# Layer 3 of a graph network on one core: node states by tile and slot, gates at the end of each chunk

## The chip, the core and the metric

The kernel runs on one core of one Trainium2 chip. The metric is the device time of one execution, in microseconds; the kernel before takes 39,711.06 us (median of 10 runs, 39,692.48 to 39,771.42). Five engines run their own instruction streams: TensorE (PE in the profile; its weight loads are PEld), VectorE (DVE), ScalarE (ACT), GpSimd (POOL) and SyncE (SP). Here POOL issues every indirect DMA (gathers and scatters of table rows by index) and SP every plain DMA.

## What is computed

A graph of 12,500 nodes with 32 features and 212,500 directed edges goes through four graph layers; each result is added to its input and layer-normalised. The sort of the edges, layers 0 to 2 and the norms are the same in both kernels, but for one column that layer 2 carries along. Layer 3 is the one that matters:

```python
out = relu(n_feat @ lin0_w.T + lin0_b); h = out
eh  = relu(e_feat @ en1_w.T + en1_b)                # edges x 128
w_e = (eh @ en2_w.T + en2_b).reshape(-1, 32, 32)    # one 32x32 matrix an edge
for _ in range(6):
    msg = einsum('ei,eio->eo', out[src], w_e)
    agg = segment_sum(msg, dst, 12500) + conv_bias
    h = gru_cell(relu(agg), h, gru_wih, gru_whh, gru_bih, gru_bhh)
    out = h
```

All of it is float32. The GRU cell is `r = sigmoid(ir+hr)`, `z = sigmoid(iz+hz)`, `n = tanh(in + r*hn)`, `h = (1-z)*n + z*h`.

## The kernel before

**Tiles, chunks, slots.** The edges, sorted by destination, are cut into 1,664 tiles of 128. A chunk is 32 tiles (`CB`), so a step has 52 chunks (`NCH`); a half is 16 tiles (`HB`). Within a tile the edges belong to a few consecutive destinations. A destination's number modulo 13 (`W`) is its slot, so a 0/1 mask of 128 edges by 13 slots, built on DVE (L848), turns the sum over edges into matmuls. A node whose edges run over several tiles is summed up by a scan along the tiles (L871). A table row for each (tile, slot), 1,664 x 13 = 21,632 rows (`SLOTS`), holds the running sum of that slot's node after that tile; `slot_end` tells for each node the row in which its sum is complete.

**One step.** The loop `For_i` runs six times over a step, whose body is written out for all 52 chunks (`conditioned` inside `slot_sum`). One half of a chunk is:

- POOL: 16 indirect gathers (L258) into `g`, three buffers. A row of the table `t3` has 64 floats (256 bytes): the state `h` of the source node and `h` times `en2_b`, the message's bias part.
- SP: one load of `eh`, 16 tiles by 128 floats, 1 MB, three buffers (L1064).
- Eight times, for a pair of tiles: DVE multiplies the state by the mask into `prod` (L1068, 128 x 2 x 32 x 13), PE makes two matmuls with `eh` as weights into `m` (L1076, two PSUM buffers), ACT copies `m` into `outer` (L1083).
- Then `flush()` runs the function `second` that the half before left behind: 32 matmuls with the blocks of `en2_i` into the four partition groups of `acc` (L1094), and after them 16 matmuls of `g[:, j, F:]` with the mask into the same `acc` (L1104). These are the last readers of `g`.

After the second half of a chunk comes `then()`: `on` (DVE, L858), `part` (ACT, L868/869), the scan (DVE, L871), `by8` (ACT, L881), four matmuls `back` (L888) that add the four partition groups and turn the result into rows by tile and slot, `o` (ACT, L896), and the write of the chunk's rows of `sums` (SP, L898).

**Between two steps.** When all chunks are done, 98 gathers fetch each node's row of `sums` by `slot_end` into `agg`; `conv_b` is added (L1004), relu (L1005), the array is transposed, and 25 groups go through the gates (L1012 to L1027: bias, two matmuls, sigmoid, tanh, five DVE operations, into `state`). Then `new_table` transposes the state, multiplies by `en2_b` (L227) and writes the whole of `t3` (L206). The next step's gathers wait for that write.

**Order.** Tile's scheduler sets the order of instructions on each engine from the program's order, a priority and the buffers of each pool; engines meet through semaphores. A float32 matmul leaves two matmul records and two weight-load records in the trace; a transpose one.

Of the kernel before, what the change touches and what calls it, by code (L numbers as in the profile page):

```python
# [62 lines left out]
R8 = 8 * W  # L64
SLOTS = R8 * J8
# [6 lines left out]
def tile_gnn(ctx: ExitStack, tc: tile.TileContext, a: dict, out: bass.AP):  # L72
# [95 lines left out]
    conv_b = rows("conv_b", a["L3_gnn_conv_bias"], F)  # L168

# [5 lines left out]
    for c in range(4):  # L175
# [9 lines left out]
    edge_h = dram.tile([P, J, EH], F32, name="edge_h", tag="edge_h")  # L185
    sums = [dram.tile([SLOTS + 1, F], F32, name=f"sums{i}", tag=f"sums{i}") for i in range(2)]
# [3 lines left out]
        for n, w in (("x", F), ("t0", F), ("t1p", F), ("t1q", F), ("t2a", F), ("t2b", F), ("t3", 2 * F))  # L190
    }

    with tc.tile_pool(name="zeros", bufs=1) as pool:
        zero = sb(pool, [P, P - NH, 2 * F], F32, "zero")
        nc.vector.memset(zero, 0.0)
        for s in scans:
            nc.sync.dma_start(s[EP : EP + 1, :], zero[0:1, 0, 0:F])
        for s in sums:
            nc.sync.dma_start(s[SLOTS : SLOTS + 1, :], zero[0:1, 0, 0:F])
        for t in tables.values():  # L200
            w = t.shape[1]
            nc.sync.dma_start(t.rearrange("(p c) f -> p c f", p=P)[:, NH:P, :], zero[:, :, 0:w])
# [62 lines left out]
    slot_end = sb(keep, [P, NH], I32, "slot_end")  # L265
    state = sb(keep, [P, C, F], F32, "state")
# [10 lines left out]
    def sort_edges():  # L277
        with ExitStack() as st:
# [41 lines left out]
            with tc.tile_pool(name="hist", bufs=1, space=PSUM) as psum:  # L320
                for k in ("s", "d"):
# [31 lines left out]
                    if k == "d":  # L353
# [5 lines left out]
                            run, ones[:, 0:1].to_broadcast([P, NH]), tot, initial=0.0, op0=ALU.mult, op1=ALU.add  # L359
                        )  # L360
# [101 lines left out]
    def all_of(pool, k, record, scattered):  # L462

        t = sb(pool, [1, record.shape[1]], I32, f"fence_{k}")
        i = nc.sync.dma_start(t, record[0:1, :])
        for s in scattered:
            after(i, s)
        return i
# [281 lines left out]
    with tc.tile_pool(name="dst", bufs=1) as dst:  # L750
# [31 lines left out]
        with tc.tile_pool(name="num", bufs=1) as work, tc.tile_pool(name="nump", bufs=2, space=PSUM) as psum:  # L782
# [40 lines left out]
            nc.vector.tensor_scalar(most, most, W - 0.5, None, op0=ALU.is_gt)  # L823
            nc.vector.tensor_copy(crowded, most[0:1, :])
# [13 lines left out]
    def slot_sum(name, rows, table, fill, agg):  # L838


        with tc.tile_pool(name=f"sl_{name}", bufs=2) as work, tc.tile_pool(
            name=f"slp_{name}", bufs=2, space=PSUM
        ) as psum:
            prev = [None]

            def one(c):
                mask = sb(work, [P, CB, W], F32, "mask", bufs=3)
                nc.vector.tensor_tensor(  # L848
                    mask,
                    slot[:, c * CB : (c + 1) * CB].unsqueeze(2).to_broadcast([P, CB, W]),  # L850
                    iota_w.unsqueeze(1).to_broadcast([P, CB, W]),
                    op=ALU.is_equal,
                )
                acc = sb(psum, [rows, CB, W], F32, "acc")

                def then():
                    on = sb(work, [rows, W, CB + 1], F32, "on")
                    nc.vector.tensor_tensor(  # L858
                        on,
                        going[0:rows, c, :].unsqueeze(1).to_broadcast([rows, W, CB + 1]),  # L860
                        iota_w[0:rows, :].unsqueeze(2).to_broadcast([rows, W, CB + 1]),
                        op=ALU.is_equal,
                    )
                    part_ = sb(work, [rows, W, CB + 1], F32, "part")
                    if prev[0] is None:
                        nc.vector.memset(part_[:, :, 0:1], 0.0)
                    else:
                        nc.vector.tensor_copy(part_[:, :, 0], prev[0][:, :, CB])  # L868
                    nc.scalar.activation(part_[:, :, 1:], acc.rearrange("p t w -> p w t"), AF.Copy)
                    s = sb(work, [rows, W, CB + 1], F32, "s")  # L870
                    nc.vector.tensor_tensor_scan(  # L871
                        s.rearrange("p w t -> p (w t)"),
                        on.rearrange("p w t -> p (w t)"),
                        part_.rearrange("p w t -> p (w t)"),
                        initial=0.0,
                        op0=ALU.mult,
                        op1=ALU.add,
                    )
                    prev[0] = s
                    by8 = sb(work, [rows, CB // 8, W, 8], F32, "by8")  # L880
                    nc.scalar.activation(  # L881
                        by8.rearrange("p b w t -> p w b t"),
                        s[:, :, 1:].rearrange("p w (b t) -> p w b t", t=8),
                        AF.Copy,
                    )
                    back = sb(psum, [R8, CB // 8, F], F32, "back", bufs=1)
                    for b in range(CB // 8):
                        nc.tensor.matmul(  # L888
                            back[:, b, :],
                            by8[:, b].rearrange("p w t -> p (w t)"),  # L890
                            stack[0:rows, :],
                            start=True,
                            stop=True,
                        )
                    o = sb(work, [R8, CB // 8, F], F32, "o")
                    nc.scalar.activation(o, back, AF.Copy)  # L896
                    n = CB // 8
                    nc.sync.dma_start(  # L898
                        table[0:SLOTS, :].rearrange("(r b) f -> r b f", r=R8)[:, c * n : (c + 1) * n, :], o
                    )  # L900

                fill(work, psum, c, mask, acc, then)

            for c in range(NCH):
                one(c)
            fill(None, None, None, None, None, None)
        for c in range(NH):
            gather(agg[:, c, :], table, slot_end[:, c : c + 1])
# [9 lines left out]
    def layer2(sum_into):  # L918

        with tc.tile_pool(name="n2", bufs=1) as n2:  # L920
# [5 lines left out]
            hid = node_array(n2, "hid")  # L926

            def conv(name, h, table, nr):

                own = sb(n2, [P, NH, F], F32, "own")  # L930
                nc.vector.tensor_tensor(own, h[:, 0:NH, :], wide(root), op=ALU.mult)
                write_table(table, own)
# [100 lines left out]

    def convolved(name, table, nr, agg):
        def fill(work, psum, c, mask, acc, then):
            if work is None:
                return
            g = sb(work, [P, CB, F], F32, "g", bufs=3)
            for j in range(CB):
                gather(g[:, j, :], tables[table], idx_d[:, c * CB + j : c * CB + j + 1])  # L1040
            for j in range(CB):
                nc.tensor.matmul(acc[:, j, :], g[:, j, :], mask[:, j, :], start=True, stop=True)
            then()

        slot_sum(f"l2{name}", F, sums[nr], fill, agg)

    def conditioned(agg):
        waiting = []

        def fill(work, psum, c, mask, acc, then):  # L1050
# [4 lines left out]
            if work is None:  # L1055
                flush()
                return
            for b in range(2):
                t0 = c * CB + b * HB
                g = sb(work, [P, HB, 2 * F], F32, "g", bufs=3)  # L1060
                for j in range(HB):
                    gather(g[:, j, :], tables["t3"], idx_d[:, t0 + j : t0 + j + 1])
                eh = sb(work, [P, HB, EH], F32, "eh", bufs=3)
                nc.sync.dma_start(eh, edge_h[:, t0 : t0 + HB, :])  # L1064
                outer = sb(work, [EH, F, HB, W], F32, "outer")
                for j in range(0, HB, 2):
                    prod = sb(work, [P, 2, F, W], F32, "prod")
                    nc.vector.tensor_tensor(  # L1068
                        prod,
                        g[:, j : j + 2, 0:F].unsqueeze(3).to_broadcast([P, 2, F, W]),  # L1070
                        mask[:, b * HB + j : b * HB + j + 2, :].unsqueeze(2).to_broadcast([P, 2, F, W]),
                        op=ALU.mult,
                    )
                    m = sb(psum, [EH, 2, 512], F32, "m")
                    for i in range(2):
                        nc.tensor.matmul(  # L1076
                            m[:, i, 0 : F * W],
                            eh[:, j + i, :],
                            prod[:, i].rearrange("p f w -> p (f w)"),
                            start=True,  # L1080
                            stop=True,
                        )
                    nc.scalar.activation(  # L1083
                        outer[:, :, j : j + 2, :].rearrange("k f t w -> k t f w"),
                        m[:, :, 0 : F * W].rearrange("k t (f w) -> k t f w", w=W),
                        AF.Copy,
                    )
                flush()

                def second(b=b, g=g, outer=outer):  # L1090
# [171 lines left out]
```

## Time and profile before

| | |
|---|---|
| median of 10 runs | 39,711.06 us |
| the profiled execution | 39,697.11 us |
| its span | 39,695.3 us |
| mean granted TensorE clock over the span | 0.685 |
| PE / PEld busy | 19,819.8 us (50%) / 11,203.6 us (28%) |
| POOL busy | 23,264.5 us (59%) |
| DVE / ACT busy | 10,520.9 us (27%) / 7,337.0 us (18%) |
| DMA, software queue (POOL's) | 723,584 packets, 512.50 MB |
| DMA, hardware queue (SP's) | 451,052 packets, 1,029.85 MB |
| layer 3 within the span | 22,660 to 39,640 us |

How to read it. The group lines have the source line, the engine, the operation, `out<-in` with its shape and the count; then the busy time in us and the mean ns of one; then the engine's idle time just before these instructions, and which event ended most of it. "issue" there means that the engine waited for no other engine and no transfer that the profile shows. A timeline line has the start, the duration, the engine and the work, and in brackets the idle time before it. A line by stretch has the stretch, its length, the busy time and the number of records of PE, PEld, DVE, ACT and POOL, the granted clock (1.00 is full speed; an idle PE shows 0.50), the share of the DMA engines and GB/s. L258, L1076 and the others are lines of the kernel before.

### The profile page before, as it was taken

How to read it: one execution, taken by the hardware profiler on the slowest of the kernel's cores; microseconds unless marked ns; L12 is line 12 of the kernel's file. 1: busy time of each engine (PE TensorE's matmuls, PEld its weight loads, DVE VectorE, ACT ScalarE, POOL GpSimd, SP SyncE). 2: the span in 40 equal slices, each digit the busy share in tenths (PEclk: the TensorE clock that was granted, in tenths of full speed). 3: DMA queues.
4: the chain of work that ended last, by engine and by line, in shares of the span. 5: the costliest groups of instructions: out<-in, count | busy, mean ns of one | idle time of the engine just before them, and what ended most of it. 6: DMA issues, size and time to landing. Idle time of an engine off the chain costs nothing. (4 is left out here: it accounts for less than half of the span.)

```text
span 39695.3 us, 317851 instructions
## 1 busy us (share of the span) xinstructions
PE 19819.8 (50%) x121935; PEld 11203.6 (28%) x121935; DVE 10520.9 (27%) x12313; ACT 7337.0 (18%) x11783; POOL 23264.5 (59%) x22620
## 2 busy tenths in 40 slices
PE   3555444400000003961111288688788688687786
PEld 3444433300000001221111144344344344343343
DVE  8333333310100003000000133333333333333333
ACT  0111111100000003110000033233233233232232
POOL 0444444477677773026666666566566566666665
PEclk6666666655555556555555588888888888888888
DMA  0000000011111113210000122122122122222222
GB/s 10 1 1 1 9 16 16 16 28 23 22 18 18 18 18 94 92 55 13 13 14 13 28 67 65 53 67 65 53 67 65 53 65 63 56 66 55 64 65 52
DMA packets 1176160, 1562.93 MB, mean 39 GB/s; under 512 B 663528, under 2 KB 885484, under 8 KB 1085804
## 3 DMA queue, kind: packets, MB, share of 16 engines
q1 hardware_dynamic: 451052, 1029.85, 7.9%
q0 software_dynamic: 723584, 512.50, 7.7%
q8 instruction: 989, 16.20, 0.2%
q14 instruction: 535, 4.38, 0.0%
HBM read 1257.04 MB, written 283.77 MB: 39 GB/s over the span
## 5 line engine op out<-in xcount | busy, mean ns | idle before, releaser
L258 POOL DMA_INDIRECT g<-t,idx_d x9984 | 10475.6, 1049 | 5565.2 <-issue 2795.9
L1076 PE MATMUL m<-prod,eh 128*128 128x416 f32 x19968 | 8365.9, 580 | 209.0 <-DVE prod L1068 132.5
L1068 DVE TENSOR_TENSOR prod<-g,mask 128x832 f32<-128x832 f32 x4992 | 5130.8, 1028 | 6316.3 <-PE m L1076 5898.3
L1083 ACT ACTIVATE outer<-m 128x832 f32<-128x832 f32 x4992 | 4507.8, 903 | 6540.9 <-PE m L1076 6216.3
L1076 PEld LDWEIGHTS m<-prod,eh 128*128 128x128 f32 x19968 | 3913.5, 213 | 3977.5 <-issue 2871.7
L1094 PE MATMUL acc<-outer,en_i 128*32 128x208 f32 x39936 | 3474.3, 359 | 1478.2 <-issue 1458.8
L382 POOL DMA_INDIRECT rec_s<-rows_s,pos x1664 | 1707.7, 1026 | 2730.5 <-DVE pos L432 2239.3
L258 POOL DMA_INDIRECT g<-t2a,idx_d x1664 | 1587.1, 954 | 2432.7 <-DMA t2a<-own 1652.8
L421 PE MATMUL place<-cur,xt 128*128 128x98 f32 x6652 | 1732.5, 354 | 2281.6 <-ACT cur L427 1217.2
L382 POOL DMA_INDIRECT rec_d<-record,row_d x1664 | 1654.4, 994 | 1993.0 <-DVE row_d L444 803.0
L1094 PEld LDWEIGHTS acc<-outer,en_i 128*32 128x32 f32 x39936 | 1528.9, 111 | 3426.7 <-issue 3113.6
L686 PE MATMUL t<-ident,gp 128*128 128x128 f32 x416 | 110.7, 441 | 4531.9 <-DMA gp<-t1p,rs 2888.1
L410 PE MATMUL same<-xt 128*128 128x128 f32 x6656 | 1661.9, 370 | 1309.9 <-issue 659.2
L848 DVE TENSOR_TENSOR mask<-slot,iota_w 128x416 f32<-128x416 bf16 x416 | 245.4, 591 | 7525.1 <-PE acc L1104 3109.9
L258 POOL DMA_INDIRECT gp<-t1p,rs x1664 | 1787.0, 1074 | 663.7 <-issue 556.4
L258 POOL DMA_INDIRECT g<-t,rs x1664 | 1770.8, 1064 | 532.5 <-issue 519.1
L258 POOL DMA_INDIRECT g<-t2b,idx_d x1664 | 1587.3, 954 | 831.0 <-issue 484.8
L258 POOL DMA_INDIRECT gq<-t1q,rs x1664 | 1763.9, 1060 | 510.3 <-issue 510.3
L421 PEld LDWEIGHTS place<-cur,xt 128*128 128x128 f32 x6652 | 1275.9, 239 | 2673.7 <-ACT cur L427 1513.8
L427 ACT ACTIVATE cur<-next 128x98 f32<-128x98 f32 x3326 | 838.5, 252 | 5419.5 <-PE next L422 2396.5
L888 PE MATMUL back<-stack,by 128*104 128x32 f32 (+1 forms) x3328 | 462.4, 290 | 2443.0 <-ACT by L881 2228.3
L410 PEld LDWEIGHTS same<-xt 128*128 128x128 f32 x6656 | 1228.7, 245 | 1468.3 <-ACT xt L407 767.2
(316 smaller groups left out, 19053.9 us busy)
## 6 DMA issues: line engine op xcount, KB each, us to landing
eh<-edge_h SPq DMA_DIRECT2D x624, 1024.0 KB
g<-t,idx_d POOLq DMA_INDIRECT x9984
edge_h<-eh SPq DMA_DIRECT2D x52, 2048.0 KB
scan<-o SPq DMA_DIRECT2D x104, 512.0 KB
ht<-h_t SPq DMA_DIRECT2D x104, 512.0 KB
rd<-rec_d SPq DMA_DIRECT2D x52, 544.0 KB
record<-in_edge_attr SPq DMA_DIRECT2D x52, 512.0 KB
rec_s<-rows_s,pos POOLq DMA_INDIRECT x1664
```

What stands on the lines that cost most here:

```text
L258: nc.gpsimd.indirect_dma_start(out=to, out_offset=None, in_=table, in_offset=bass.IndirectOffsetOnAxis(ap=idx, axis=0))
L382: i = nc.gpsimd.indirect_dma_start(out=to, out_offset=bass.IndirectOffsetOnAxis(ap=idx, axis=0), in_=data, in_offset=None)
L410: nc.tensor.matmul(same[:, j, :], xt[:, j, :], xt[:, j, :], start=True, stop=True)
L421: nc.tensor.matmul(place[:, j, :], xt[:, j, :], cur, start=False, stop=True)
L427: nc.scalar.activation(cur, nxt, AF.Copy)
L686: nc.tensor.transpose(t[:, g, :], gp[:, jj : jj + 4, :].rearrange("p j f -> p (j f)"), ident)
L848: nc.vector.tensor_tensor(mask, slot[:, c * CB : (c + 1) * CB].unsqueeze(2).to_broadcast([P, CB, W]), iota_w.unsqueeze(1).to_broadcast([P, ...
L888: nc.tensor.matmul(back[:, b, :], by8[:, b].rearrange("p w t -> p (w t)"), stack[0:rows, :], start=True, stop=True,)
L1068: nc.vector.tensor_tensor(prod, g[:, j : j + 2, 0:F].unsqueeze(3).to_broadcast([P, 2, F, W]), mask[:, b * HB + j : b * HB + j + 2, :].unsq ...
L1076: nc.tensor.matmul(m[:, i, 0 : F * W], eh[:, j + i, :], prod[:, i].rearrange("p f w -> p (f w)"), start=True, stop=True,)
L1083: nc.scalar.activation(outer[:, :, j : j + 2, :].rearrange("k f t w -> k t f w"), m[:, :, 0 : F * W].rearrange("k t (f w) -> k t f w", w=W ...
L1094: nc.tensor.matmul(af[q * F : (q + 1) * F, b * HW : (b + 1) * HW], en2_i[:, i, :], outer[:, i].rearrange("k t w -> k (t w)"), start=i < 4, ...
```

## The change

Layer 3 of the usual path is written anew as `layer3_tiles`; the general path for crowded graphs keeps the old `layer3`.

- The node states live in two tables, `states[0]` and `states[1]`, with a row for each (tile, slot), like `sums`. At the start `h` is scattered to `states[0]` by `slot_end` with 98 indirect DMAs, and a read that waits for all of them (`all_of`) follows. The set-up at the start of the kernel fills `states[0]` with zeros.
- The gathers of a step read these tables directly, by the row number of the source node, `idx_t`. The rows have 32 floats (128 bytes); there is no bias half. `idx_t` is made in layer 2: its tables get a 33rd column with `slot_end`, and the chunk's copy of that column is kept.
- The bias part now goes by the sum of the states: 16 mask matmuls sum the gathered states into `ssum`, ACT copies them to `ss`, the 32 matmuls with `en2_i` follow, and four matmuls with `en2_b` (`by4`) add the bias part to `acc`. In `second` the mask matmuls, the last readers of `g`, thus come first. `g` has four buffers.
- Each chunk ends with its own gates: `stack` adds the four partition groups into `ft` (by feature), relu with `conv_bias` gives `mt`, the chunk's 4 x 104 old rows (`old`, loaded by SP at the start of the chunk) are transposed to `ht`, one bias matmul and eight GRU matmuls fill `gates`, then sigmoid, tanh and five DVE operations, and SP writes the chunk's rows of the next table. Every row of the table gets a state, of running sums too; rows of unfinished sums are never gathered.
- The loop runs three times over two steps, `a` from `states[0]` to `states[1]` and `b` back. The 98 gathers by `slot_end` remain once, behind the loop.
- `m` keeps two PSUM buffers; `acc`, the sums `states`, `ft` and `gates` have one each (in the kernel before `acc` has two and `back` one).
- `crowded` is set as well when the graph has nodes without a row (`lacking`).

The core of the diff (`running` and `mask_of` hold the old lines of `slot_sum` up to `by8`, whose layout is now `b, (w t)`; the pair loop in `half` is the old one with `g[:, j : j + 2, :]`):

```diff
-        for n, w in (..., ("t2a", F), ("t2b", F), ("t3", 2 * F))
+        for n, w in (..., ("t2a", F + 1), ("t2b", F + 1), ("t3", 2 * F))
...
     def convolved(name, table, nr, agg):
+        def fill(work, c, mask, acc):
+            g = sb(work, [P, CB, F + 1], F32, "g", bufs=3)
             for j in range(CB):
                 gather(g[:, j, :], tables[table], idx_d[:, c * CB + j : c * CB + j + 1])
+            if name == "a":
+                nc.vector.tensor_copy(idx_t[:, c * CB : (c + 1) * CB], g[:, :, F])
...
+    def layer3_tiles():
...
+            for c in range(NH):
+                i = nc.gpsimd.indirect_dma_start(
+                    out=states[0],
+                    out_offset=bass.IndirectOffsetOnAxis(ap=slot_end[:, c : c + 1], axis=0),
+                    in_=h[:, c, :],
+                    in_offset=None,
+                )
...
+            all_of(n3, "states", states[0], scattered_, F32)
+
+        def gates(work, psum, c, by8, old, new):
+            t = sb(psum, [F, B8, R8], F32, "ft")
+            nc.tensor.matmul(
+                t.rearrange("f b r -> f (b r)"), stack, by8.rearrange("p b r -> p (b r)"), start=True, stop=True
+            )
+            mt = sb(work, [F, B8, R8], F32, "mt")
+            nc.scalar.activation(mt, t, AF.Relu, bias=conv_col[:, 0:1])
+            t = sb(psum, [F, B8, R8], F32, "ft")
+            for b in range(B8):
+                nc.tensor.transpose(t[:, b, :], old[:, b, :], ident[0:R8, 0:R8])
+            ht = sb(work, [F, B8, R8], F32, "ht")
+            nc.scalar.activation(ht, t, AF.Copy)
+            t = sb(psum, [R8, B8, 4, F], F32, "gates")
+            nc.tensor.matmul(
+                t.rearrange("r b k f -> r (b k f)"), ones2[:, 0:R8],
+                gru_b.rearrange("b c k f -> b (c k f)"), start=True, stop=False, skip_group_check=True,
+            )
+            for b in range(B8):
+                tb = t[:, b].rearrange("r k f -> r (k f)")
+                nc.tensor.matmul(tb, mt[:, b, :], gru_i[0:F, 0, :], start=False, stop=False, skip_group_check=True)
+                nc.tensor.matmul(tb, ht[:, b, :], gru_h[0:F, 0, :], start=False, stop=True, skip_group_check=True)
+            rz = sb(work, [R8, B8, 2, F], F32, "rz")
+            nc.scalar.activation(rz, t[:, :, 0:2, :], AF.Sigmoid)
...
+            nc.sync.dma_start(by_chunk(new, c), d)
+
+        def step(k, old_, new):
...
+                def half(c, b, mask, old, sums_):
+                    t0 = c * CB + b * HB
+                    g = sb(work, [P, HB, F], F32, "g", bufs=4)
+                    for j in range(HB):
+                        gather(g[:, j, :], old_, idx_t[:, t0 + j : t0 + j + 1])
...
+                    flush()
+
+                    def second():
+                        if b == 0:
+                            sums_.append(sb(psum, [P, CB, W], F32, "acc"))
+                            sums_.append(sb(psum, [P, GC, W], F32, "states"))
+                        acc, ssum = sums_
+                        for j in range(HB):
+                            q = j % 4
+                            nc.tensor.matmul(
+                                ssum[q * F : (q + 1) * F, b * HB // 4 + j // 4, :],
+                                g[:, j, :], mask[:, b * HB + j, :], start=True, stop=True,
+                            )
+                        n = HB // 4
+                        ss = sb(work, [P, n, W], F32, "ss")
+                        nc.scalar.activation(ss, ssum[:, b * n : (b + 1) * n, :], AF.Copy)
+                        af = acc.rearrange("p t w -> p (t w)")
+                        for i in range(F):
...
+                        by4 = acc.rearrange("p (g q) w -> p g q w", q=4)
+                        for q in range(4):
+                            nc.tensor.matmul(
+                                by4[q * F : (q + 1) * F, b * n : (b + 1) * n, q, :],
+                                en2_b[q * F : (q + 1) * F, q, :], ss[q * F : (q + 1) * F],
+                                start=False, stop=True, skip_group_check=True,
+                            )
+                        if b == 1:
+                            prev[0], by8 = running(work, P, c, acc, prev[0])
+                            gates(work, psum, c, by8, old, new)
+
+                    waiting.append(second)
+
+                for c in range(NCH):
+                    mask = mask_of(work, c)
+                    old = sb(work, [R8, B8, F], F32, "old", bufs=3)
+                    nc.sync.dma_start(old, by_chunk(old_, c))
+                    sums_ = []
+                    half(c, 0, mask, old, sums_)
+                    half(c, 1, mask, old, sums_)
+                flush()
...
+            with tc.For_i(0, STEPS // 2, 1):
+                step("a", states[0], states[1])
+                step("b", states[1], states[0])
+        for c in range(NH):
+            gather(state[:, c, :], states[0], slot_end[:, c : c + 1])
...
     with tc.If(reg == 0) as cmp:
         layer2(convolved)
-        layer3(conditioned)
+        layer3_tiles()
```

## The prediction, made before the changed kernel ran

> **What bounds the kernel now.** I read the page's groups, then the timeline and the busy time by stretch inside one chunk of layer 3, then the stretch between two steps. Layer 3 runs from 22,660 us to 39,640 us: six steps of 52 chunks. The group view names its three large parts.
>
> ```profile
> L258 POOL DMA_INDIRECT g<-t,idx_d x9984 | 10475.6, 1049 | 5565.2 <-issue 2795.9 <-PE acc L1104 1985.1 <-DVE mask L848 721.7
> L1076 PE MATMUL m<-prod,eh 128*128 128x416 f32 x19968 | 8365.9, 580 | 209.0 <-DVE prod L1068 132.5 <-issue 38.3 <-DMA eh<-edge_h 22.3
> L1104 PE MATMUL acc<-mask,g 128*32 128x13 f32 x19968 | 846.1, 208 | 1277.9 <-issue 1217.7 <-DMA g<-t,idx_d 59.4
> ```
>
> POOL waits 1985 us for the mask matmuls of L1104, and ahead of those PE is idle for 1,278 us, 1,218 of it "issue": it waits there for nothing visible. A float32 matmul leaves two records (a transpose one); I count records, each with its weight load. The timeline (start, duration, engine, work, idle before) shows both waits meeting.
>
> ```profile
> 37281.60 0.29 PE L1104 MATMUL acc<-mask,g 128*32 128x13 f32 x4 [0.89 <-issue]
> 37281.91 0.95 POOL L258 DMA_INDIRECT g<-t,idx_d  x1 [0.30 <-issue]
> 37282.32 0.18 PE L1104 MATMUL acc<-mask,g 128*32 128x13 f32 x1 [0.43 <-issue]
> 37283.04 0.28 PE L1104 MATMUL acc<-mask,g 128*32 128x13 f32 x3 [0.54 <-issue]
> 37283.78 0.18 PE L1104 MATMUL acc<-mask,g 128*32 128x13 f32 x1 [0.46 <-issue]
> 37284.48 0.54 PE L1104 MATMUL acc<-mask,g 128*32 128x13 f32 x22 [0.52 <-issue]
> ...
> 37285.59 0.95 POOL L258 DMA_INDIRECT g<-t,idx_d  x1 [2.74 <-PE acc L1104]
> ```
>
> While POOL gathers, PE gets a few matmuls every 0.72 us. POOL's last gather ends at 37282.85; 1.6 us later 22 come in 0.54 us; POOL, which needs their buffer, restarts. The same by stretch (length, then busy us and records of PE, weight loads, DVE, ACT, POOL; clock; DMA):
>
> ```profile
> 37262.30:37274.60 12.30, 12.30 (x38) 6.06 (x36) 7.90 (x9) 7.16 (x9) 9.78 (x9) 0.91 0.16 29
> 37274.64:37277.88 3.24, 3.19 (x57) 1.89 (x56) 1.03 (x1) 0.91 (x1) 2.60 (x3) 1.00 0.71 209
> 37277.88:37284.40 6.52, 2.38 (x18) 0.92 (x18) 0.00 (x0) 0.00 (x0) 3.79 (x4) 0.79 0.29 95
> 37284.40:37285.02 0.62, 0.54 (x23) 0.51 (x23) 0.00 (x0) 0.00 (x0) 0.00 (x0) 0.50 0.00 0
> 28069.40:28076.10 6.70, 6.64 (x193) 5.71 (x192) 0.00 (x0) 0.90 (x1) 0.00 (x0) 1.00 0.01 2
> ```
>
> After the `m` matmuls (first line) PE has some 56 in hand and runs them in 3.2 us; then it crawls, 18 in 6.52 us = 2.8 per us, until POOL stops. The last line is a step's end, where POOL gathers nothing: 193 run without a hole. So I read the loop as two engines in turn: 16 gathers last 21.2 us (37236.9 to 37258.1), PE crawls meanwhile, finishes the masks in the open gap of 2.7 us, and POOL goes on. A chunk takes 48.97 us (median over the starts of `back`). Layer 2 gathers rows of 128 bytes, as the changed layer 3 will, and crawls too: 12 in 5.0 us.
>
> ```profile
> 18503.86 0.37 PE L1042 MATMUL acc<-mask,g 128*32 128x13 f32 x4 [0.54 <-issue]
> 18504.43 0.94 POOL L258 DMA_INDIRECT g<-t2a,idx_d  x1 [0.30 <-issue]
> 18505.27 0.35 PE L1042 MATMUL acc<-mask,g 128*32 128x13 f32 x4 [1.03 <-issue]
> ...
> 18508.85 0.18 PE L1042 MATMUL acc<-mask,g 128*32 128x13 f32 x1 [1.82 <-issue]
> ```
>
> **What goes: the stretch between steps.** From the last `m` of step 1 (25,238.6) to the first of step 2 (25,507.8) are 269 us.
>
> ```profile
> 25238.70:25251.20 12.50, 9.42 (x203) 7.26 (x196) 1.05 (x1) 2.16 (x4) 0.00 (x0) 0.94 0.02 6
> 25251.20:25373.40 122.20, 1.07 (x2) 0.00 (x0) 0.00 (x0) 0.00 (x0) 92.62 (x98) 0.50 0.10 13
> ...
> 25389.50:25464.00 74.50, 73.79 (x155) 25.68 (x155) 36.98 (x123) 17.81 (x49) 0.00 (x0) 0.98 0.00 0
> ...
> 25486.70:25507.80 21.10, 0.00 (x0) 0.02 (x1) 3.70 (x8) 0.00 (x0) 6.50 (x7) 0.50 0.76 307
> ```
>
> The 98 gathers, the gates and the table go. What stays: 12.5 us of trailing matmuls, one chunk's gates, its write, and 8.3 us from first gather to first `m`. The gates' chain after the scan I put at 14 us (`ft` 1.4 cold, two evictions 1.0, transposes 1.4, 16 matmuls 4, sigmoid 0.4, tanh 0.3, five DVE operations 1.5, hand-overs), the write at 2. 37 us, so 232 saved five times: 1,160. At the end the 98 gathers remain, once (122 us): 12.5 + 14 + 2 + 122 + 4 = 155 against 262, saves 107. At the start 98 scatters are new: not in the trace with this row; the gathers' 1.25 us each gives 122, the sort's scatters (L382: 1026 ns busy on average, with a hole of 0.3 to the next) the same; with the fence 4, less the first table (25): costs 101. Zero rows for `states` (2.8 MB), `idx_t`'s 52 copies, gathers of 132 bytes in layer 2: bounds 0 and 60, I take 16. Net: -1,150.
>
> **What comes: 32 matmul records a chunk.** `by4` 16, bias 2, `ft` 2, transposes 4, GRU 16, less `back` 8; 264 become 296. The order of the built program shows the gates spread over the first three pairs of `m` of each second half, so ACT's six and DVE's five small operations hide behind `m` matmuls: uncovered, ACT's would cost about 2 us (two copies of 416 wide at 0.52 as `part`, a sigmoid 0.38, a tanh 0.31, two small ones, less the 0.28 of `o`) and DVE's 1.5 (five at 0.29, as the gates' own now). No table switch is added in a chunk. On SP the row write stands where that of `sums` stood, ahead of two `eh` loads, and waits for the gates; `eh` has three buffers and is loaded half a chunk ahead, so it hides; `old` is one 53 KB load. PE is left. From outside: all 32 in the open gap (22 in 0.54 us) cost 0.8 us a chunk; all crawling (2.8 per us) 11.4.
>
> Which, depends on the order: the matmuls that release `g` now stand first, so the gap opens ahead of the 64 with `en2_i` (now L1094) and not of `m`. I walk one chunk; t = 0 is the release.
> - POOL restarts at 0.6 and slows PE from about 1.9. By then 33 of L1094 are done and 56 in hand; the other 31 and 8 `by4` are done at 4.2 with 23 in hand. `m` takes 13.3 (some cold) to 17.5, the next release comes at about 19: POOL, busy until 21.8, has its next buffer already and gathers on, to 43.2.
> - The second half starts at 19 with nothing in hand: 72 records of L1094 and `by4` need 25.7 us of crawl, to 44.7, when POOL has just stopped. Then 32 `m` (11.1) and 24 gate matmuls (3.2) follow at their own speed, and 32 masks (0.6): 59.6.
>
> The gap is thus spent on `m`, which cannot use it. With 3.1 per us (38 in 12.30 us, the `m` stretch) the crawl passes 8 more `m` and the chunk is 56.8. I take the middle, 58.2: +9.2 us, times 312 = +2,870. Sum: 39,695 - 1,150 + 2,870 = 41,415 us; the profiled run was 39,697, the median 39,711, so 41,430.
>
> [...]
>
> **Rivals.**
> 1. The gap still falls well (each half's release waits for its own 16 gathers, as now). For it: that is the rhythm of today, and `g` has four buffers for three. Against: the two halves no longer have equal work. Then +0.8 us: 39,711 - 1,150 + 250 = 38,810. It decides below 3.7 us a chunk (1,150/312).
> 2. The crawl has another cause that goes with the wide rows or the late masks. POOL paces alone: 42.4 + 1 us, -5.6: 36,800. Against: layer 2's rows.
> 3. The gates' waits show as well: `ft` waits for `by8` (0.52 + 1.05 + 0.55 us after the last `by4`), the transposes for `mt`, since `ft` has one buffer; 2 to 4 us a chunk more, about 42,400 and up.
>
> That the gates do not leave the stretch between steps is excluded: no 98 gathers stand in the changed loop.
>
> **Chances.** Forecast 0.58, rival 1 0.26, rival 2 0.05, rival 3 0.11. The forecast's own range is 40,300 (54.5 us) to 42,600 (62). With rival 1 held, 38,750 to 42,600; what is left out is rival 2, most of rival 3's upper part and the edges, about 0.2. What cannot be told from no change is 0.2%, 80 us, a chunk between 3.4 and 3.9 us longer: 0.03. Faster 0.29, slower 0.68.
>
> **What would show it.** Between steps about 37 us in place of 269. In the loop: `m` starts alternating in distance, POOL gathering 32 times without a gap and then waiting 10 us or more for the masks, the 64 matmuls with `en2_i` with "issue" holes in one half of two. I am wrong if POOL still stops after every 16 gathers, or if those 64 run through while POOL gathers.

## The result, and the profile after

The changed kernel takes 44,847.3 us (median of 8 runs, 44,805 to 44,897), the kernel before 39,715.0 us in the same comparison: ratio 1.129, 95% interval 1.1283 to 1.1302. It is slower by 5,132 us, and the time lies above the range given (38,750 to 42,600 us). The kernel before itself takes either 39,480 to 39,750 us or 34,555 to 34,610 us, the same throughout one series of runs (kernels measured side by side on one chip), and nothing in the profiles says why; so each number below stands beside the time of the kernel before from its own series.

The spans differ by 44,848.9 - 39,695.3 = 5,154 us. What was to go did go. Between two steps there are 33.1 us on average in place of 269.4 (five times: -1,182); from the last `m` to the end of the span 181 in place of 304 (-123); the first `m` comes 151.5 later. Sum -1,153. So the 312 chunks cost +6,307, 20.2 us each: from one `ft` to the next 69.8 us pass (median), where a chunk took 48.97.

The groups of the changed kernel (busy, mean ns of one, idle before and what ended it):

```profile
L269 POOL DMA_INDIRECT g<-states,idx_t x9984 | 9784.1, 980 | 12012.7 <-PE states L1179 5379.7 <-PE acc L1192 3381.8 <-issue 2952.2
L1149 DVE TENSOR_TENSOR prod<-g,mask 128x832 f32<-128x832 f32 x4992 | 5088.8, 1024 | 12276.5 <-remote 7727.7 <-PE m L1157 3082.6 <-issue 356.7
L1157 PE MATMUL m<-prod,eh 128*128 128x416 f32 x19968 | 9278.6, 617 | 5553.6 <-DVE prod L1149 5207.9 <-issue 238.3 <-ACT outer L1164 85.5
L1164 ACT ACTIVATE outer<-m 128x832 f32<-128x832 f32 x4992 | 4452.4, 900 | 11732.8 <-remote 7336.6 <-PE m L1157 3535.8 <-issue 274.9
L1192 PE MATMUL acc<-outer,en_i 128*32 128x208 f32 x39936 | 2091.5, 341 | 111.6 <-issue 111.2
```

Two groups of the kernel before, for comparison:

```profile
L1068 DVE TENSOR_TENSOR prod<-g,mask 128x832 f32<-128x832 f32 x4992 | 5130.8, 1028 | 6316.3 <-PE m L1076 5898.3 <-issue 115.9 <-DMA g<-t,idx_d 115.1
L1094 PE MATMUL acc<-outer,en_i 128*32 128x208 f32 x39936 | 3474.3, 359 | 1478.2 <-issue 1458.8
```

POOL waits 12,013 us where it waited 5,565. The 64 records with `en2_i` (now L1192) no longer have holes: 112 us of idle in all, 1,478 before. DVE and ACT now wait 7,700 and 7,300 us each for something that the profile can't name ("remote"). The timeline of one half shows what:

```profile
35024.46 0.44 PE L1179 MATMUL states<-mask,g 128*32 128x13 f32 x32
...
35024.74 3.54 PE L1192 MATMUL acc<-outer,en_i 128*32 128x208 f32 x64
...
35025.61 0.94 POOL L269 DMA_INDIRECT g<-states,idx_t  x1 [18.01 <-PE acc L1192]
...
35029.91 0.26 PE L1202 MATMUL acc<-ss,en_b 32*32 32x52 f32 x2 [1.15 <-issue]
...
35031.36 2.28 PE L1157 MATMUL m<-prod,eh 128*128 128x416 f32 x6 [0.29 <-issue]
...
35044.33 0.94 POOL L269 DMA_INDIRECT g<-states,idx_t  x1 [0.30 <-issue]
35048.49 1.96 DVE L1149 TENSOR_TENSOR prod<-g,mask 128x832 f32<-128x832 f32 x2 [22.89 <-remote]
35048.55 1.68 ACT L1164 ACTIVATE outer<-m 128x832 f32<-128x832 f32 x2 [22.90 <-remote]
35049.63 0.50 PEld L1157 LDWEIGHTS m<-prod,eh 128*128 128x128 f32 x2 [16.66 <-ACT outer L1164]
...
35060.66 0.44 PE L1179 MATMUL states<-mask,g 128*32 128x13 f32 x32
...
35061.80 1.30 POOL L269 DMA_INDIRECT g<-states,idx_t  x1 [16.52 <-PE acc L1192]
```

The masks run at 24.46 and release `g`; POOL gathers from 25.61 to 45.27. PE's records go on: the 64, `by4`, two pairs of `m`, the last ending at 33.64. Yet ACT, whose next work is to copy those `m`, and DVE, which needs the buffer that they free, start at 48.5, 3.2 us after POOL's last gather. Then the other pairs of the half run in 12 us, with POOL idle, and the next masks release it. The same half by stretch (length; busy us and records of PE, weight loads, DVE, ACT, POOL; clock; DMA):

```profile
35024.46:35028.28 3.82, 3.82 (x97) 3.09 (x97) 1.03 (x1) 1.07 (x2) 2.07 (x3) 1.00 0.72 234
35028.28:35033.64 5.36, 3.76 (x17) 1.74 (x16) 0.00 (x0) 0.00 (x0) 4.14 (x5) 1.00 0.20 50
35033.64:35048.49 14.85, 0.00 (x0) 0.00 (x0) 0.00 (x1) 0.00 (x0) 8.89 (x10) 0.62 0.09 11
35048.49:35060.66 12.17, 11.00 (x25) 5.33 (x25) 7.08 (x7) 6.18 (x7) 0.00 (x0) 0.76 0.00 0
```

For 14.85 us nothing but POOL works; for 12.17 us everything but POOL. A half takes 35.5 us (median between masks), and the two add up: 20.0 of gathers, 3.1 until DVE starts again, and 12.4 for the rest. Counted over layer 3, 4,953 of the 4,992 `prod` of the kernel before start while POOL gathers, of the changed kernel's 737. ACT starts its copy of a pair of `m` more than 10 us after the pair's last record 614 times out of 4,992 in the changed kernel, never in the kernel before.

The trace also holds the times at which PE's semaphore was incremented; ACT's copies of `m` that begin after a wait start by the median 0.023 us after such an increment (4,306 copies), so this counter is what ACT goes by here. Some are missing from the whole trace (30,349 for 31,970 records that carry one), but this stretch has 39 of each. Matched in order, they are late:

```
record starts   line     increment seen
35025.35        L1192    35025.70
35026.45        L1192    35029.91
35027.94        L1192    35041.30
35029.97        L1202    35048.38
35030.55        L1157    35048.42
35033.13        L1157    35048.55
35050.49        L1157    35051.40
```

At the two ends of these rows an increment comes 0.01 us after the record's end (0.35 us after the start of the record of L1192 at 35025.35, 0.5 to 0.9 us for the `m` from 35050.49 on). Here the lag grows to 18 us while POOL gathers (19.6 us, from the record's end, for a `by4` between these rows). From 35032.80 to 35046.94 the increments come 1.4 us apart, or two or three times that; then six come within 0.21 us, four of them of `m` matmuls whose records are 0.7 to 1.2 us apart. So what is late is mostly the signal, not the matmul.

### The profile page after: what moved, and what is told of

It is laid out like the page before. It is cut to its first block, busy times and chain, and to the rows that moved or that the text cites. A ratio compares the mean times of both kernels' runs of the same rounds, so it can differ in the third digit from the quotient of the medians.

```text
span 44848.9 us, 335014 instructions
## 1 busy us (share of the span) xinstructions
PE 20129.5 (45%) x130344; PEld 11782.8 (26%) x130344; DVE 10504.9 (23%) x12888; ACT 7700.1 (17%) x13037; POOL 22190.9 (49%) x22228
## 5 line engine op out<-in xcount | busy, mean ns | idle before, releaser
L269 POOL DMA_INDIRECT g<-states,idx_t x9984 | 9784.1, 980 | 12012.7 <-PE states L1179 5379.7
L1157 PE MATMUL m<-prod,eh 128*128 128x416 f32 x19968 | 9278.6, 617 | 5553.6 <-DVE prod L1149 5207.9
L1157 PEld LDWEIGHTS m<-prod,eh 128*128 128x128 f32 x19968 | 4175.4, 226 | 10233.7 <-ACT outer L1164 6337.5
L1192 PE MATMUL acc<-outer,en_i 128*32 128x208 f32 x39936 | 2091.5, 341 | 111.6 <-issue 111.2
L1192 PEld LDWEIGHTS acc<-outer,en_i 128*32 128x32 f32 x39936 | 1728.2, 110 | 241.1 <-issue 236.9
L914 PE MATMUL back<-ident,by 32*104 32x32 f32 x832 | 165.4, 359 | 2712.9 <-ACT by L892 2447.8
L881 ACT ACTIVATE part<-acc 128x416 f32<-128x416 f32 (+1 forms) x416 | 214.5, 516 | 6513.5 <-remote 5688.1
```

What stands on the lines that cost most here:

```text
L269: nc.gpsimd.indirect_dma_start(out=to, out_offset=None, in_=table, in_offset=bass.IndirectOffsetOnAxis(ap=idx, axis=0))
L914: nc.tensor.matmul(back[:, b, :], by8[:, b, :], ident[0:F, 0:F], start=True, stop=True)
L1157: nc.tensor.matmul(m[:, i, 0 : F * W], eh[:, j + i, :], prod[:, i].rearrange("p f w -> p (f w)"), start=True, stop=True,)
L1192: nc.tensor.matmul(af[q * F : (q + 1) * F, b * HW : (b + 1) * HW], en2_i[:, i, :], outer[:, i].rearrange("k t w -> k (t w)"), start=i < 4, ...
```

## The experiments

The edits are shown shortened, `...` for what is left out. Theory A, called A' once the runs had shown that it acts in some series only: the mask matmuls, put first, start POOL's gathers as the 64 records run; PE's increments come late while POOL gathers, so the next `m` waits for the end of the gathers. Theory B: the gates' chain costs the 20 us.

| series: kernel before, us | runs (us) |
|---|---|
| 1: 34,569 | masks last 33,910 (0.981, 0.979 to 0.983); no gates 33,629; before with masks first 34,607; one plain load 30,636 |
| 2: 39,484 | changed kernel 42,413 (1.074, 1.072 to 1.076) |
| 3: 34,596 | masks last 33,962 (0.982, 0.980 to 0.983); before with masks first 34,596; no gates 33,614; SP row loads 30,751 |
| 4: 39,745 | masks last 39,648 (0.998, 0.997 to 0.999) |
| 5: 34,608 | before with masks first 34,643 (1.001, 1.000 to 1.003) |
| 6: 39,496 | changed kernel 42,275 (1.071, 1.069 to 1.073); before with masks first 42,054; no gates 41,508 |
| 7: 39,747 | SP row loads 33,962; changed kernel 44,889 (1.129, 1.128 to 1.131) |
| 8: 34,555 | POOL row loads 30,708; changed kernel 33,799 (0.978, 0.977 to 0.980) |

### The masks last (series 1, 3, 4)

```diff
                         acc, ssum = sums_
-                        for j in range(HB): matmul(ssum[...], g[:, j, :], mask[...])
-                        ss = ...; activation(ss, ssum[...], AF.Copy)
                         for i in range(F): matmul(af[...], en2_i[:, i, :], outer[:, i], ...)
+                        for j in range(HB): matmul(ssum[...], g[:, j, :], mask[...])
+                        ss = ...; activation(ss, ssum[...], AF.Copy)
                         by4 = acc.rearrange(...)
```

> The changed kernel with one thing undone: in second() the 16 mask matmuls, which release g, stand behind the 32 matmuls with en2_i again. Theory A (the release of g ahead of the 64 records starts POOL's gathers at the wrong moment: PE's completions are held back while POOL gathers, the m of the next half waits for them, and each half becomes 20 us of gathers plus 3 plus 13 of m = 36): the halves fall back to about 25 us, a chunk to 49-53 us from 69.8, the time to 38,300-39,900 us. Theory B (the gates' chain with its single PSUM buffers is what costs the 20 us a chunk): the time stays above 44,000 us.

In series 1, 33,910 us: below the expected band, but there the kernel before is 5,100 us faster too, and the test says nothing. Series 3 gave the same. In series 4 the kernel before took 39,745 us:

> The changed kernel with the mask matmuls behind the 32 with en2_i, a third time, since the chips of the first two calls did not show late increments at all. Where the kernel before takes 39,400-39,800 us: theory A' 38,000-39,600 us (0.96 to 1.00 of the kernel before, against 1.07 to 1.13 with the masks first), theory B (the gates) above 41,500 us. Where it takes 34,570 us: 33,900 us again.

39,648 us, a ratio of 0.998: A' fell just outside its band of time and inside that of the ratio, and B is out. Against the changed kernel of series 7 (44,889 us, with the kernel before equal to 2 us) the order of two blocks is worth 5,241 us, 16.8 us a chunk; a chunk takes 51.4. DVE's group in series 4:

```profile
L1149 DVE TENSOR_TENSOR prod<-g,mask 128x832 f32<-128x832 f32 x4992 | 5112.3, 1026 | 5693.3 <-PE m L1157 3868.7 <-remote 724.9 <-issue 613.6
```

"remote" falls from 7,728 to 725 us, and 4,392 of 4,992 `prod` start while POOL gathers.

### The order alone, in the kernel before (series 1, 3, 5, 6)

```diff
                 def second(b=b, g=g, outer=outer):
+                    extra = sb(psum, [P, CB, W], F32, "extra", bufs=1)
+                    for j in range(HB): matmul(extra[...], g[:, j, F:], mask[...], start=True, stop=True)
                     for i in range(F): matmul(af[...], en2_i[:, i, :], outer[:, i], ...)
-                    for j in range(HB): matmul(acc[...], g[:, j, F:], mask[...], start=False, stop=True)
```

> The kernel before with one thing of the change done alone: the 16 mask matmuls stand ahead of the 32 with en2_i. They write a PSUM tile of their own, and the bias part of the message is left out of the sum, so the output is not the reference's. Theory A: a half goes from 24.4 to about 36-38 us (21.2 of gathers, 3, and 13 of m), a chunk from 49 to 70-75 us, the time to 46,000-48,000 us. Theory B: no gates stand in the chunk, the time stays within 39,400-40,200 us.

> The kernel before with the mask matmuls first, into a tile of their own; the bias part is left out of the sum. Where the kernel before takes 39,400-39,800 us: theory A' 42,500-47,000 us, rival C (the place alone does nothing) 39,300-40,300 us. Where it takes 34,570 us: 34,600 us by both, as three times before.

In series 1, 3 and 5 hardly a difference (34,596 to 34,643 us). In series 6, one run of 42,054 us against 39,496: 8.2 us a chunk, less than A' gave, but rival C is out: the place of the masks costs without gates and without rows of 128 bytes. The pattern is close to the one forecast. By stretch:

```profile
33001.43:33044.02 42.59, 25.93 (x162) 14.13 (x153) 10.88 (x12) 9.36 (x12) 33.04 (x31) 0.81 0.24 64
33044.02:33054.72 10.70, 9.78 (x74) 4.62 (x76) 7.10 (x8) 6.22 (x7) 0.00 (x1) 0.94 0.05 9
33054.72:33097.29 42.57, 29.39 (x191) 13.56 (x181) 10.34 (x12) 8.46 (x11) 33.08 (x32) 0.79 0.27 74
```

Here POOL gathers two halves in a run (42.6 us) and then waits 10.7, as the prediction drew it. How often depends on the wait that is counted as a stop: with waits of under 1 us left out, 147 of its runs have 32 gathers and 308 have 16; with those of under 3 us left out, 285 and 26. Between two such pairs of halves POOL mostly waits 10 to 20 us.

### The gates left out (series 1, 3, 6)

```diff
     def gates(work, psum, c, by8, old, new):
-            t = sb(psum, [F, B8, R8], F32, "ft")
...
-            nc.sync.dma_start(by_chunk(new, c), d)
+            nc.sync.dma_start(by_chunk(new, c), old)
```

> The changed kernel without its gates: everything from ft to d is left out, the old rows are written to the next table as they are, so the output is not the reference's. Theory A: each half stays at about 34-36 us, a chunk loses 0 to 4 us, the time is 43,500-44,850 us. Theory B: a chunk falls to about 50 us and the time to 38,500-39,500 us.

> The changed kernel without its gates, the old rows written on as they are. Where the kernel before takes 39,400-39,800 us: theory A' 40,500-44,800 us, 0 to 6 us a chunk less than the changed kernel in the same call; theory B 38,000-39,300 us. Where it takes 34,570 us: 33,600 us again.

Series 6: one run of 41,508 us against 42,275 of the changed kernel beside it, 2.5 us a chunk. B is out.

### Without POOL's gathers (series 1, 3, 7, 8)

```diff
                     for j in range(HB):
-                        gather(g[:, j, :], old_, idx_t[:, t0 + j : t0 + j + 1])
+                        nc.sync.dma_start(g[:, j, :], by_part[:, (t0 + j) % (SLOTS // P), :])
```

`by_part` is the table as 128 partitions by 169 rows. In series 1 one load of 2,048 rows took the place of the 16; in series 8 POOL issued the 16 row loads (`nc.gpsimd`).

> The changed kernel with the 16 gathers of a half replaced by one plain load of 2,048 rows of the same table on SP's queue; the rows are not those of the source nodes, so the output is not the reference's. POOL has nothing to do in the loop. Theory A: completions are prompt, a half is m (11 to 13 us) and 3 to 7 us for the rest, a chunk 32-42 us, the time 33,000-36,200 us. Theory B: POOL is not the pace, the chunk stays above 60 us and the time above 42,000 us.

> The changed kernel with each of the 16 gathers of a half replaced by a plain DMA of 128 rows of 128 bytes from the same table on SP's queue: as many descriptors and bytes, but POOL does nothing; the rows are not those of the source nodes, so the output is not the reference's. If POOL's own part of a gather holds PE's increments back (A' in the narrow sense), they are prompt here: a chunk of 32-45 us and 33,500-37,500 us where the kernel before takes 39,400-39,800. If the small transfers do it, whoever issues them, the increments lag as before and a chunk stays above 55 us.

> The changed kernel with each of the 16 gathers of a half replaced by a plain DMA of 128 rows of 128 bytes of the same table on SP's queue; the rows are not those of the source nodes. Where the kernel before takes 39,400-39,800 us: if POOL's own part of a gather holds PE's increments back, they are prompt here, a chunk is 32-45 us and the time 33,500-37,500 us; if the small transfers do it, a chunk stays above 55 us and the time above 41,000 us. Where the kernel before takes 34,570 us: 30,750 us again.

Series 1 and 3 gave 30,636 and 30,751 us, below the bands, since the stages ahead of layer 3 are shorter there as well (the first `m` starts at 19,514 and 19,575 us, at 22,790 in series 7). Series 7 is the test: one run of 33,962 us beside 44,889 of the changed kernel. A chunk takes 34.83 us, with the masks first, the gates in place, and as many transfers of as many bytes. The groups there:

```profile
L1158 PE MATMUL m<-prod,eh 128*128 128x416 f32 x19968 | 7487.1, 525 | 22.6 <-DMA eh<-edge_h 20.4 <-DVE prod L1150 1.0
L1150 DVE TENSOR_TENSOR prod<-g,mask 128x832 f32<-128x832 f32 x4992 | 5115.3, 1025 | 3446.9 <-PE m L1158 2073.8 <-DMA g<-states 1368.7 <-DMA eh<-edge_h 1.7
```

No "remote" is left among what ended DVE's idle time, and PE hardly waits ahead of `m`. So transfers as such don't hold the increments back here. What is left is the indirect gather as POOL issues it: POOL's own part, or the queue that it uses.

> The changed kernel with each of the 16 gathers of a half replaced by a plain DMA of the same 128 rows of 128 bytes as in the runs with SP's row loads, but issued by POOL; the rows are not those of the source nodes. Where the kernel before takes 39,400-39,800 us: if any DMA that POOL prepares holds PE's increments back, a chunk stays above 50 us and the time above 39,000 us; if only the indirect form does, 33,900-36,500 us, as with SP's (33,962 us). Where the kernel before takes 34,570 us: 30,700-34,500 us.

30,708 us, but in a series with a kernel before of 34,555 us, where this tells nothing. Whether every DMA that POOL issues has the effect, or the indirect form alone, stays open.

### The changed kernel again (series 2, 6, 7, 8)

> The changed kernel once more, since in the runs just made the kernel before took 34,569 us and not 39,715. Theory A' (what costs is PE's semaphore increments that come late while POOL gathers, and this happens on one chip and not on another): where the kernel before takes 39,700 us this takes 44,850 us again (1.129); where it takes 34,570 us this takes 33,700-34,300 us (0.975 to 0.992), within 1% of the version with the masks last, since the order then costs nothing. Theory B (the gates cost 20 us a chunk): slower than the kernel before on every chip, by 8% or more.

> The changed kernel as it is. Where the kernel before takes 34,570 us (increments prompt): theory A' 33,800-34,200 us, a ratio of about 0.98; any theory in which the order or the gates cost by themselves: above 35,500 us. Where it takes 39,400-39,800 us: 42,200-44,900 us again.

> The changed kernel as it is. Where the kernel before takes 34,570 us (increments prompt): theory A' 33,800-34,200 us, a ratio of about 0.98; any theory in which the order or the gates cost by themselves: above 35,500 us. Where it takes 39,400-39,800 us: 42,200-44,900 us again.

Where the kernel before takes 39,747 us the loss came back (1.129); where it takes 39,480 to 39,500, for which the first expectation names no time, it is about half of that (1.071 and 1.074, a chunk 60.6 to 61.5 us); where it takes 34,555 us the change gains 2.2% (33,799 us, at the lower edge of the band). The groups of that last run:

```profile
L269 POOL DMA_INDIRECT g<-states,idx_t x9984 | 10870.4, 1089 | 3188.0 <-issue 2915.0 <-DMA g<-states,idx_t 96.0 <-DVE mask L858 82.9
L1149 DVE TENSOR_TENSOR prod<-g,mask 128x832 f32<-128x832 f32 x4992 | 5125.5, 1030 | 7304.4 <-DMA g<-states,idx_t 4773.5 <-PE m L1157 2263.3 <-PE states L1179 230.2
```

POOL never stops within a step (its waits are the 0.3 us between gathers), DVE waits for rows, and 4,986 of 4,992 `prod` start while POOL gathers; ACT's `part` starts 0.07 us after the last `by4` record, 5.6 in the first profile of the changed kernel. POOL is the pace: 44.6 us a chunk.

One count over the whole of layer 3 puts the runs side by side: how often ACT starts its copy of a pair of `m` more than 10 us after the pair's last record (of 4,992). It is 612 in the changed kernel of series 7 and 602 in that of series 6, 27 with the masks last in series 4, and none in the changed kernel of series 8 and with SP's row loads in series 7.

## Why the prediction was wrong

**The stretch between steps** was right: -1,153 against -1,150. The parts were 33 us for 37 between steps, -123 for -107 at the end, +151 for +117 at the start. Over all steps they were off by -22, -16 and +34 us, so it is partly luck that the sum is this close.

**The 9.2 us a chunk** were wrong: 20.2. The step that failed is in the walk: "the other 31 and 8 `by4` are done at 4.2 with 23 in hand. `m` takes 13.3 (some cold) to 17.5, the next release comes at about 19". By the records the first part came close (`by4` ended 5.7 us after the masks began). But I took a record in the timeline for work that is done: what the others wait for is the increment, and it came 24 us after the masks. So two of the eight pairs of `m` were issued beside the gathers, and no other engine could use them before these had ended; the next release came at 36.2 and not at 19, POOL had no second buffer to go on with, and every half, not one of two, became gathers plus `m`. The marks set in the prediction say the same: POOL still stops after every 16 gathers, and the 64 run through without holes. That the change would be slower came true, at three times the loss forecast (5,132 us for 1,719). The rhythm forecast, two halves gathered in a run, was found in the kernel before with the masks first instead, at 56.9 us a chunk (median) beside the 58.2 forecast.

**The crawl** of PE in the kernel before was real, and its link to POOL's gathers too (18 records in 6.52 us beside gathers, 193 in 6.70 us at a step's end without them); its cause was most likely misread as a shortage of instructions. In the kernel before the increments lag too: the record of L1094 at 37255.71 ends at 37256.05 and has its increment at 37259.96, 1.9 us after POOL's last gather, and those of the 16 masks follow 0.042 us apart. These matmuls stand in the trace already, so a shortage of instructions does not explain that their signals are late. That slow signals also hold up the records behind them, which would look like a slow feed from the issue side, is argued and not shown. How many records PE can have in hand is not shown either, though the prediction reckoned with 56: the first hole of over 0.5 us comes after 56 records with `en2_i` in the timeline of the kernel before (from 37274.64), and after 102 records (32, 64 and 6) in the half of the changed kernel above.

**Rival 1** (the gap falls well) is what the masks last restore: 39,648 us, 3.4 us a chunk over the kernel before, beside the break-even of 3.7 worked out. **Rival 2** (POOL alone paces) is what happens where the increments are prompt: its sign held there (0.978), with a chunk of 44.6 us for its 43.4; its time can't be compared. **Rival 3** can't be priced apart: leaving out the whole of the gates, not their waits alone, is worth 2.5 us a chunk in series 6, beside its 2 to 4, a small part of the loss.

**Left open**: why the increments are late in some series and prompt in others (one chip number showed both), why the loss has two sizes where they are late (`part` starts, by the median, 3.4 us after the last `by4` record in series 2 and 6, 5.6 to 6.3 us in the first profile and series 7), and which of POOL's doings delays them.

## What to carry to other kernels

A matmul's record in the timeline did not say here when the other engines learned that it was done: the increments came up to 19.6 us after the record's end. That is read from the first instruction of another engine that waits for it, and idle time with no nameable releaser on two engines at once (7,728 us on DVE, 7,337 us on ACT) was the sign that signals were late. Before a release of a gather's buffer is moved forward, look at what the gathers will then run beside: where the increments were late here, they belonged beside the slow, wide `m` (617 ns a record in the first profile), not beside the 72 short records of `en2_i` (341 ns) and `by4` (215 ns): 39,648 us in series 4 against 44,889 us in series 7. The version with the masks last is the one to keep if a loss must be excluded: 0.998 and 0.981 of the kernel before in the two conditions, where the changed kernel as it is has 1.129 and 0.978.

## What the runs showed of the hardware

- In the first profile of the changed kernel PE's semaphore increments lag behind the records while POOL issues indirect gathers, by up to 19.6 us in the half shown, and catch up 0.042 us apart once the gathers end. In series 6 and 7, where it is slower too, 602 and 612 of ACT's 4,992 copies start more than 10 us after the last record of their pair.
- The granted clock is lower in the stall and behind it: 1.00 in the 9.18 us ahead of it, 0.62 over the 14.85 us of waiting and 0.76 in the 12.17 us of `m` behind it; `m` records take 617 ns on average, 580 before.
- With SP's row loads a chunk takes 34.83 us in series 3 and in series 7, though the kernel before takes 34,596 and 39,747 us there: without the gathers, the two conditions do not differ in layer 3.
